# Two graph layers on one core: four walk blocks instead of three, first-walk rows on GpSimd's queue, the last row pair by halves, and layer-1 pools split by place

## The chip, the cores and the metric

The kernel runs on one core of one Trainium2 chip. Its time is the device time of one execution in microseconds (us). The engines are named as in the profile: PE is TensorE's matmul side and PEld its weight loads, DVE is VectorE, ACT is ScalarE, POOL is GpSimd, and SP is SyncE, which only issues DMAs. ACT and POOL can issue DMAs too, from queues of their own.

## The reference, cut to what matters

The input is `x` (2708 rows of 256) and a sparse 2708 x 2708 matrix `adj`. Two layers follow each other.

```python
# layer 0, two steps n = 0, 1
R = adj + eye(N);  R = R / R.sum(-1)                  # a row-stochastic walk matrix
A  = top_p_attention(Xa, W1, W2, W3)                  # softmax of q k^T, cut to the 0.9 nucleus, renormalised
Xf = R @ Xf                                           # the walk
Xa = A @ Xa                                           # the attention
Z += Xf @ U1[n].T + Xa @ U2[n].T
x  = layernorm(x + layernorm(X + Z) * g + b)
# layer 1: graph attention, 4 heads of 64
e  = leaky_relu(s_i[:, None] + s_j[None, :])          # masked where adj (with its diagonal) is 0
x  = layernorm(x + softmax(e) @ Wh)
```

Each walk is a dense product of the 2708 x 2708 matrix with 256 columns, each attention step makes the scores, searches the cut of the nucleus in every row, transposes the probabilities and multiplies them with 256 columns, and layer 1 is a masked product of the same size for four heads.

## The kernel before, in words

The 2708 rows are 22 row tiles: 16 of 128 rows and 6 of 110. Two neighbouring tiles make a pair, so there are 11 pairs (`PAIRS`).

**The walk** (`walks`, from line 1021) does the product of one pair of row tiles with all columns in seven phases, a Strassen scheme of 2 x 2 blocks (Winograd's form). Each phase multiplies one block matrix of 11 tiles (`D11`, `S2`, `A12`, `S3`, `S1`, `D22`, `S4`; `A12` comes from `adj`, the others were mixed during the first attention step and lie in DRAM) with one half of the columns (`B11`, `T2`, `B21`, `T3`, `T1`, `T4`, `B22`). A phase is 11 products, which the trace shows as 22 matmul instructions. A phase's block is 704 KB. The buffers of the blocks come from the pool `adjp`, which has three; the block of phase `at + 2` is requested when phase `at` begins (line 1067), into the buffer of phase `at - 1`. SP issues these transfers (line 681, `get`; line 669 for `A12`, `fetch`). There are 77 phases in the first walk and 77 in the second.

The operands `B..` and `T1` lie in `xe`, the terms `T2`, `T3` and `T4` in `xm`, which held the layer's input until the first attention step was done with it. A column of ones in `xe` and one in `t2` give the row sums: in the first walk the phases 0 to 2 are 129 columns wide, and lines 1090 and 1094 take the reciprocals. Lines 1086 to 1102 take each phase's sum out of PSUM, some on ACT, most on DVE. Two PSUM banks (`walk0`, `walk1`) change turns, so phase 4 of a pair can begin when ACT has copied phase 2's result (line 1092), phase 5 when DVE has added phase 3's (line 1096), and the next pair's phase 0 when DVE has added phase 5's (line 1100).

When a row tile of the first walk is done, `after_walk0` (line 1143) scales it and adds a term on POOL (lines 1146, 1148), and SP stores it to DRAM (line 1149, `xmd`). The term (`ca`) is fetched by SP (line 1046, in `beside`), asked for in phase 3. The last pair is not stored: POOL writes it straight into `xe` (line 1151), both halves of the columns of both tiles, after the pair's phase 6. `return_rows` (line 1114) brings the other rows from `xmd` into `xe` in three parts, as the operands come free. `reblend` (line 1130) then makes `T3`, `T2` (DVE, lines 998 and 1000), `T1` and `T4` (POOL, lines 1002 and 1004) for the second walk. The second walk's phase 0 waits in the program's order for both tiles of the last pair to be written, and its later phases for the blends.

**The attention** (`step`, line 1252) goes row tile by row tile. Each has six groups of up to four 128-column parts: a transpose on PE (line 258), a copy on ACT (line 263, `eT`), a product (line 276, `att`). After each group `slot` (line 1237) advances the other work by one step: the search for the cut of later rows (lines 787 to 960: exponentials and counts on ACT, a short chain of one-column operations on POOL from line 794 to 840, the sorting on DVE), what follows finished rows, and then up to 12 products of the walk. Between the two attention steps there is a stretch in which slots run one after another with 14 products each (line 1367 and 1372): there the walk runs without attention beside it.

The program writes out the order of PE, ACT, DVE and POOL by hand (`manual_schedule` with those four engines), so each of these engines does its instructions in the order of the program text. SP is not among them: a planner orders its DMAs by when it reckons that they can start, and SP then works through that list one by one. An SP transfer whose wait isn't over holds everything behind it.

`finish` (line 1206) ends a row tile of the second walk: it stores the row (line 1222, `xd`) and then runs `sources` (line 158), which makes layer 1's values and stores them (line 183, `v`). For the last three tiles it puts their first term into `x_late` (line 1049), behind a small POOL memset (line 1042).

**Layer 1** (`layer1`, line 1446) takes the same buffers over: its pools open when layer 0's pools close. In each of three spans (1024, 1024 and 660 columns) it goes over the 22 tiles `j`: the mask block of `j` comes by SP (line 238, `neighbours`, into `adjp`), ACT makes it 0 or 1 (lines 239 and 240, Sign and Square), DVE makes the weights `pt` for four heads (line 1540, four instructions), and PE multiplies (line 1552 values, line 1562 denominators). The pool `pj` holds the weights of three `j`, `ps_v` the six PSUM banks of the sums, `keep1` the 22 value tiles. The first two masks are asked for in the last attention tile, after its group 4 (line 1278, `early`). Layer 1's stretched-out rows of the span (`e<-shared`, `r<-shared`) come by lines 216 and 224. At `(g, i) == (0, 12)` SP brings the rows stored in `xd` back into `xe` (line 1615, 2 MB and 330 KB), for the residual sum that begins in the second span.

Of the kernel before, what the change touches and what calls it, by code (L numbers as in the profile page):

```python
# [45 lines left out]
def kernel(  # L46
# [57 lines left out]
    nc.gpsimd.memset(xe[:, :, HALF : HALF + 1], 1.0)  # L104
# [439 lines left out]
    def fast_layer0(ep, adjp):  # L544
# [89 lines left out]
        p1, y1, y2 = (spare_u[:, k * (HALF + 1) : (k + 1) * (HALF + 1)] for k in range(3))  # L634
        u_rows = u_sb[:, 1].rearrange("p c s d -> p (c s) d")
        lines = [u_rows[:, k, :] for k in range(4)]
        lines += [spare_u[:, c : c + D] for c in (3 * HALF + 3, 3 * HALF + 3 + D)]
# [338 lines left out]
        def halves_of(t, m):  # L976
# [5 lines left out]
        t2 = flat[:, PAIRS * HALF : PAIRS * (D + 1)].rearrange("p (j c) -> p j c", c=HALF + 1)  # L982
        t4 = flat[:, PAIRS * (D + 1) : PAIRS * (D + 1 + HALF)].rearrange(
            "p (j c) -> p j c", c=HALF
        )

# [5 lines left out]
        def blend(name, j0, j1, k):  # L992
# [3 lines left out]
            u3, u2, u4 = t3[:k, j0:j1], t2[:k, j0:j1, 0:HALF], t4[:k, j0:j1]  # L996
# [13 lines left out]
            "T1": lambda j, k, w: xe[:k, 2 * j, second],  # L1010
            "T2": lambda j, k, w: t2[:k, j, 0:w],
# [9 lines left out]
        def walks():  # L1021
# [6 lines left out]
            def load(s, i, n):  # L1028
                blk = new_block(rows[2 * i])
                key = PHASES[n][0]  # L1030
                if key == "A12":
                    fetch(blk, 2 * i, 1)
                else:
                    get(key, i, blk)
                return blk

            def beside(s, t):
# [7 lines left out]
                if not s:  # L1045
                    nc.sync.dma_start(ca[:m], c1[t][:m])
                    return ca, None
# [9 lines left out]
            blocks = [load(*queue[0]), load(*queue[1])]  # L1057
            walking.append(True)
            yield
            for at, (s, i, n) in enumerate(queue):  # L1060
# [3 lines left out]
                while s and (unfinished or (n and blending)):  # L1064
                    yield True
                blk = blocks.pop(0)
                if at + 2 < len(queue):
                    blocks.append(load(*queue[at + 2]))
# [5 lines left out]
                if n == 3:  # L1074
                    aside = {t: beside(s, t) for t in (a, b)}
                w = HALF + 1 if s == 0 and n < 3 else HALF
                ac = use[bank][:m, :w]
                for j in range(PAIRS):
# [5 lines left out]
                    if j == PAIRS - 1:  # L1084
                        if n == 0:
                            nc.scalar.copy(p1[:m, :w], ac)
                        elif n == 1:
                            nc.vector.tensor_add(y1[:m, :w], ac, p1[:m, :w])
                            if s == 0:
                                nc.vector.reciprocal(rinv[:m, b : b + 1], y1[:m, HALF : HALF + 1])  # L1090
                        elif n == 2:
                            nc.scalar.copy(xa[:m, :HALF], ac[:, :HALF])
                            if s == 0:
                                nc.vector.reciprocal(rinv[:m, a : a + 1], ac[:, HALF : HALF + 1])
                        elif n == 3:
                            nc.vector.tensor_add(y2[:m, :HALF], ac, p1[:m, :HALF])
                        elif n == 4:
                            nc.vector.tensor_add(xb[:m, HALF:], ac, y2[:m, :HALF])
                        elif n == 5:
                            nc.vector.tensor_add(xb[:m, :HALF], ac, y2[:m, :HALF])  # L1100
                        else:
                            nc.vector.tensor_add(xa[:m, HALF:], ac, y1[:m, :HALF])
                        for t, xw, last in ((b, xb, 5), (a, xa, 6)):
                            if n == (6 if (s, i) == (0, PAIRS - 1) else last):
                                if s == 0:
                                    unfinished.add(t)
                                doing.append((after_walk0, finish)[s](t, xw[:m], *aside[t]))
                                next(doing[-1])
                        if (s, i) == (0, PAIRS - 1) and n in (2, 4, 6):
                            return_rows(n)  # L1110
# [3 lines left out]
        def return_rows(n):  # L1114

            odd, cols = {2: (None, slice(0, HALF)), 4: (0, second), 6: (1, second)}[n]
# [9 lines left out]
            if n == 6:  # L1126
                blending.append(True)
                doing.append(reblend())

        def reblend():  # L1130
# [3 lines left out]
            while unfinished:  # L1134
# [8 lines left out]
        def after_walk0(t, xw, ca, _):  # L1143
# [3 lines left out]
            if t < NT - 2:  # L1147
                nc.gpsimd.tensor_add(xw, xw, ca[:m])
                nc.sync.dma_start(xmd[:m, t], xw)
            else:  # L1150
                nc.gpsimd.tensor_add(
                    halves_of(t, m), xw.rearrange("p (h c) -> p h c", h=2),
                    ca[:m].rearrange("p (h c) -> p h c", h=2),
                )
            unfinished.remove(t)
# [50 lines left out]
        def finish(t, xw, ca, cb):  # L1206
# [12 lines left out]
            if not late:  # L1219
                yield  # L1220
                yield from norms(t, xt, ca)
                nc.sync.dma_start(xd[:m, t], xt)
                yield from sources(t, rowp, free_bank, src=xt)


        going, doing, unfinished, stored = [], [], set(), set()
        early, walked, blending, begun = [], [], [], []
# [24 lines left out]
        def step(s, cur, spend):  # L1252
            turned_first = None
            for t in range(NT):
# [11 lines left out]
                def between(n):  # L1266
# [11 lines left out]
                    if s and (t, n) == (NT - 1, len(groups) - 2):  # L1278

                        early.extend(neighbours(0, j, adjp) for j in first[:2])  # L1280
                    if (s, t) == (0, NT - 1):
# [4 lines left out]
                        if n == 2:  # L1286
                            nc.gpsimd.memset(t2[:, :, HALF : HALF + 1], 1.0)
# [158 lines left out]
    def layer1(ep, adjp, r=None, verdict=None, early=()):  # L1446
        l1 = ExitStack()

        pp, rp, pj, keep = (
            l1.enter_context(tc.tile_pool(name=name, bufs=bufs))  # L1450
            for name, bufs in (("pp", 2), ("rp", 1), ("pj", 1), ("keep1", 1))
        )
        DEEP = 3
# [284 lines left out]
```

## Time and profile before

| | |
|---|---|
| median of 3 runs | 1554.12 us (1552.58 to 1556.42) |
| profiled execution, its own time | 1554.5 us |
| its span | 1552.5 us |
| PE busy | 1496.7 us (96%) |
| DVE busy | 1297.9 us (84%) |
| ACT busy | 800.4 us (52%) |
| POOL busy | 611.0 us (39%) |
| mean granted TensorE clock | 0.987 |

The span lies 2 us below the time of the same execution, so a difference of spans can be read as a difference of times. PE is busy nearly all the time, which makes its few idle stretches the thing to look at, together with the stretches in which its clock was granted at half. The stages, by the times at which their lines run: the first attention step with the mixing of the blocks up to 440 us, the walk alone to 521 us, the second attention step with the rest of the first walk up to 790 us and with the second walk from there to 1197 us, the last attention groups to 1205 us, and layer 1 to the end.

Columns of the profile's lines: a wait is "who waited, for whom: us in total, times, longest". A timeline line is "start, duration, engine, line, operation, out<-in, shape, count, [idle time before it, and what ended it]". A line that counts several instructions starts with the first and ends with the last.

### The profile page before, as it was taken

The numbers are of one execution on the slowest core, as the hardware profiler recorded it, in microseconds if no ns is written. First come the engines' busy times: TensorE is split into PE (matmuls) and PEld (weight loads), VectorE is DVE, ScalarE is ACT, GpSimd is POOL, SyncE is SP. The second block draws the span as 40 slices with busy tenths as digits, with TensorE's granted clock in tenths as the row PEclk, the third lists the DMA queues.
The fourth block names the chain that finished last, engine by engine and source line by source line (L and its number), as shares of the span: only waits on it lengthen the run. The fifth ranks groups of instructions, "written<-read, shape, count | busy, mean of one in ns | idle before, by whom it ended". The sixth has DMA issues, their size and how long they took to land.

```text
span 1552.5 us, 29929 instructions
## 1 busy us (share of the span) xinstructions
PE 1496.7 (96%) x10537; PEld 1068.9 (69%) x10537; DVE 1297.9 (84%) x3763; ACT 800.4 (52%) x1472; POOL 611.0 (39%) x1016
## 2 busy tenths in 40 slices
PE   8999999999998999999989999999998999999995
PEld 4477777777787889988878888888887323333342
DVE  4599999999525878888889998999893998999995
ACT  3444444444335456656645666666641444456474
POOL 2267777865023223222343454545432220035133
PEclk9999999999998999999999999999999999999998
DMA  6198988894037655544555555555556445334331
GB/s 171 57 273 260 287 272 260 263 260 154 12 117 221 182 163 160 172 154 143 168 157 167 173 175 172 183 164 157 146 169 198 123 118 169 96 106 132 86 108 46
DMA packets 208010, 255.97 MB, mean 165 GB/s; under 512 B 42151, under 2 KB 171949, under 8 KB 207851
## 3 DMA queue, kind: packets, MB, share of 16 engines
q1 hardware_dynamic: 198042, 239.68, 51.4%
q0 software_dynamic: 3648, 9.26, 1.9%
q10 hardware_dynamic: 6161, 5.03, 1.1%
q8 instruction: 85, 1.39, 0.4%
q14 instruction: 74, 0.61, 0.1%
HBM read 190.10 MB, written 62.44 MB: 163 GB/s over the span
## 4 chain that ended last, share of the span: by engine, by line
PE 83%; DVE 8%; POOL 3%; ACT 2%; DMA 2%; issue 2%; ACTq 0%; DVEq 0%; SPq 0%; POOLq 0%
PE att L276 24%; PE walk L1080 20%; PE acc L1552 11%; PE lg L783 7%; PE tr L258 6%; PE acc L1562 6%; DVE pt L1540 3%; PE walk L1181 2%; PE walk L1197 2%; DMA blk<-S 1%; PE walk L753 1%; PE lg L170 1%; DVE top L906 1%; DVE work L908 1%; ACT junk L808 1%
## 5 line engine op out<-in xcount | busy, mean ns | idle before, releaser
L808 ACT ACTIVATE junk<-e,minus,rth 128x2708 bf16<-128x2708 f32 (+1 forms) x88 | 232.9, 2647 | 49.7 <-POOL rth L840 48.9
L1080 PE MATMUL walk<-xe,blk 128*128 128x128 f32 (+7 forms) x1936 | 242.4, 277 | 12.5 <-DMA blk<-S 4.6
L263 ACT COPY eT<-tr 128x512 f32<-128x512 f32 (+5 forms) x264 | 141.4, 536 | 218.4 <-PE tr L258 215.8
L1080 PEld LDWEIGHTS walk<-xe,blk 128*128 128x128 f32 (+3 forms) x1936 | 230.7, 188 | 28.6 <-issue 16.8
L276 PE MATMUL att<-ba,eT 128*128 128x256 f32 (+3 forms) x968 | 231.3, 380 | 0.0
L276 PE MATMUL att<-xm,eT 128*128 128x256 f32 (+3 forms) x968 | 230.8, 379 | 0.3 <-ACT xa L1270 0.3
L1552 PE MATMUL acc<-pt,v 128*32 128x512 f32 (+3 forms) x2112 | 218.3, 547 | 3.7 <-ACT xa L1270 3.1
L1080 PE MATMUL walk<-xm,blk 128*128 128x128 f32 (+6 forms) x1452 | 188.0, 280 | 7.8 <-DMA blk<-S 6.3
L1540 DVE SCALAR_TENSOR_TENSOR pt<-e,tj,blk 128x1024 f32<-128x1024 f32 (+3 forms) x176 | 184.4, 1113 | 10.6 <-PE att L276 7.8
L1080 PEld LDWEIGHTS walk<-xm,blk 128*128 128x128 f32 (+3 forms) x1452 | 178.0, 191 | 20.9 <-issue 12.5
L276 PEld LDWEIGHTS att<-ba,eT 128*128 128x128 f32 (+3 forms) x968 | 170.2, 187 | 21.5
L276 PEld LDWEIGHTS att<-xm,eT 128*128 128x128 f32 (+3 forms) x968 | 169.6, 186 | 22.0 <-ACT xa L1270 0.7
L787 ACT ACTIVATE e<-lg 128x1024 f32<-128x1024 f32 (+1 forms) x132 | 121.0, 921 | 112.9 <-PE lg L783 107.0
L1552 PEld LDWEIGHTS acc<-pt,v 128*32 128x32 f32 (+1 forms) x2112 | 70.6, 110 | 136.0 <-issue 111.3
L258 PE MATMUL tr<-ident,e 128*128 128x128 f32 (+3 forms) x968 | 148.3, 272 | 4.0 <-ACT eT L263 4.0
L258 PEld LDWEIGHTS tr<-ident,e 128*128 128x128 f32 (+3 forms) x968 | 112.0, 139 | 46.2 <-issue 26.7
L1562 PE MATMUL acc<-pt,sb 128*32 128x512 f32 (+3 forms) x1056 | 112.8, 542 | 0.0
L1540 DVE SCALAR_TENSOR_TENSOR pt<-r,tj,blk 128x1024 f32<-128x1024 f32 (+1 forms) x88 | 109.9, 1313 | 1.2 <-issue 0.6
L888 DVE MAX8 cand<-scr 128x8 f32<-128x97 f32 (+1 forms) x616 | 102.9, 247 | 0.0
L888 DVE MAX8 cand<-e 128x8 f32<-128x170 f32 (+1 forms) x352 | 85.8, 323 | 20.4 <-ACT e L787 20.3
L239 ACT ACTIVATE blk<-blk 128x1024 f32<-128x1024 f32 (+3 forms) x66 | 63.2, 959 | 75.5 <-DMA blk<-in_adjT_dram 65.9
L906 DVE MAX8 top<-work 128x8 f32<-128x128 f32 (+3 forms) x242 | 82.4, 340 | 8.3
(265 smaller groups left out, 2206.4 us busy)
## 6 DMA issues: line engine op xcount, KB each, us to landing
blk<-in_adjT_dram SPq DMA_DIRECT2D x72, 512.0 KB
blk<-S SPq DMA_DIRECT2D x64, 512.0 KB
blk<-D SPq DMA_DIRECT2D x32, 512.0 KB
blk<-in_adjT_dram SPq DMA_DIRECT2D x27, 440.0 KB
blk<-S SPq DMA_DIRECT2D x64, 165.0 KB
blk<-S SPq DMA_DIRECT2D x24, 440.0 KB
D<-blk SPq DMA_DIRECT2D x16, 512.0 KB
S<-scr SPq DMA_DIRECT2D x16, 512.0 KB
```

Source lines behind the costliest of these rows:

```text
L258: nc.tensor.transpose(tr[: rows[t], q, :m], e[:m, off[t] : off[t + 1]], ident[:m, :m])
L263: copy(eT[:k, : len(grp), :m], tr[:k, : len(grp), :m])
L276: nc.tensor.matmul(acc, eT[: rows[t], q, :m], value(t), start=(t == 0), stop=(t == NT - 1),)
L783: nc.tensor.matmul(lg[:m, h, :w], qT[part, cols], kT[s][part, c0 : c0 + w], start=True, stop=True,)
L787: nc.scalar.activation(halves[:m, :, c0 : c0 + w], lg[:m, :, :w], AF.Exp, accum_out=zp[:m, n : n + 1],)
L808: nc.scalar.activation(junk[:m], e[:m], func, scale=rth, bias=minus1[:m], accum_out=acc)
L888: nc.vector.max(cand[:, n, :], src[:m, n * size : min(N, (n + 1) * size)])
L906: nc.vector.max(top[:, k : k + 8], work if k else flat)
L1080: nc.tensor.matmul(ac, blk[:k, j, :], MOVING[name](j, k, w), start=start and j == 0, stop=j == PAIRS - 1, skip_group_check=True,)
L1540: nc.vector.scalar_tensor_tensor(pt[:k, :gw], targets[g][h // 2][:k, h % 2, :gw], tj[:k, j, h : h + 1], bar, op0=ALU.max, op1=ALU.mult,)
L1552: nc.tensor.matmul(acc[h // 2][c][to : to + SIDE, :w], v[j][:k, h, o : o + SIDE], probs[n][h][:k, c0 : c0 + w], **at,)
L1562: nc.tensor.matmul(acc[2][c][h * SIDE : (h + 1) * SIDE, :w], sb[:k, j, h : h + 1].to_broadcast([k, SIDE]), probs[n][h][:k, c0 : c0 + w], **at,
```

## The change

- **Four walk blocks, three ahead.** `t2` loses its column of ones, so `t3`, `t2` and `t4` fill three quarters of `xm`, and the last quarter is a fourth block buffer (`fourth`), taken by every fourth phase. The block of phase `at + 3` is requested when phase `at` begins.
- **Row sums.** `xe` gets a second column of ones behind its second half. The row sum of the odd tile comes with phase 4 (`S1`, `T1`) instead of phase 1, so the phases 0, 2 and 4 are 129 wide, and that tile's reciprocal is taken after phase 4. `p1`, `y1`, `y2` lose their extra column.
- **First-walk rows by GpSimd's queue.** The term's load (now in phase 0 of the pair) and the store to `xmd` are issued by POOL, 22 and 20 DMAs.
- **The last pair by halves.** `last_rows` scales and adds each half of each of the last two tiles as it is done (after phases 2 and 5, and both second halves after phase 6). The second walk's phase 0 waits only for the first halves; later phases still wait for the blends.
- **`finish`** stores `xd` after `sources` instead of before it.
- **Layer 1.** `pj` becomes three pools of one, `ps_v` six pools of one bank, and the first four value tiles get a pool of their own (`keep2`), so each waits for what lay in its own place. The two early masks are asked for after group 3 instead of group 4. A small POOL memset on `xe` is put ahead of the transfers of line 1615.

```diff
     xe = const.tile([P, NT, D + 2], F32, name="xe")
-    nc.gpsimd.memset(xe[:, :, HALF : HALF + 1], 1.0)
+    for one in (HALF, D + 1):
+        nc.gpsimd.memset(xe[:, :, one : one + 1], 1.0)
...
         t3 = flat[:, : PAIRS * HALF].rearrange("p (j c) -> p j c", c=HALF)
-        t2 = flat[:, PAIRS * HALF : PAIRS * (D + 1)].rearrange("p (j c) -> p j c", c=HALF + 1)
...
+        t2, t4 = (
+            flat[:, k * PAIRS * HALF : (k + 1) * PAIRS * HALF].rearrange("p (j c) -> p j c", c=HALF)
+            for k in (1, 2)
         )
+        fourth = flat[:, 3 * PAIRS * HALF :]
...
             def load(s, i, n):
-                blk = new_block(rows[2 * i])
+                if (s * PAIRS * 7 + i * 7 + n) % 4 == 3:
+                    blk = compact(fourth, rows[2 * i])
+                else:
+                    blk = new_block(rows[2 * i])
...
                 if not s:
-                    nc.sync.dma_start(ca[:m], c1[t][:m])
+                    nc.gpsimd.dma_start(ca[:m], c1[t][:m])
                     return ca, None
...
-            blocks = [load(*queue[0]), load(*queue[1])]
+            AHEAD = 3
+            blocks = [load(*queue[at]) for at in range(AHEAD)]
...
-                while s and (unfinished or (n and blending)):
+                while s and (owing & {(t, 0) for t in (NT - 2, NT - 1)} or (n and blending)):
                     yield True
                 blk = blocks.pop(0)
-                if at + 2 < len(queue):
-                    blocks.append(load(*queue[at + 2]))
+                if at + AHEAD < len(queue):
+                    blocks.append(load(*queue[at + AHEAD]))
...
-                if n == 3:
+                if n == (3 if s else 0):
                     aside = {t: beside(s, t) for t in (a, b)}
-                w = HALF + 1 if s == 0 and n < 3 else HALF
+                w = HALF + 1 if s == 0 and n in (0, 2, 4) else HALF
...
+                        if (s, i) == (0, PAIRS - 1):
+                            if n in (2, 4, 6):
+                                return_rows(n)
+                            for t, xw, h in {
+                                2: ((a, xa, 0),), 5: ((b, xb, 0),), 6: ((b, xb, 1), (a, xa, 1))
+                            }.get(n, ()):
+                                owing.add((t, h))
+                                doing.append(last_rows(t, xw[:m], aside[t][0], h))
                                 next(doing[-1])
...
             nc.gpsimd.tensor_scalar(xw, xw, rinv[:m, t : t + 1], None, op0=ALU.mult)
...
+            nc.gpsimd.tensor_add(xw, xw, ca[:m])
+            nc.gpsimd.dma_start(xmd[:m, t], xw)
+            rows_kept.append(t)
+
+        def last_rows(t, xw, ca, h):
+            m, cols = rows[t], slice(h * HALF, (h + 1) * HALF)
+            yield
+            nc.gpsimd.tensor_scalar(
+                xw[:, cols], xw[:, cols], rinv[:m, t : t + 1], None, op0=ALU.mult
+            )
+            nc.gpsimd.tensor_add(halves_of(t, m)[:, h, :], xw[:, cols], ca[:m, cols])
+            owing.remove((t, h))
...
                 yield from norms(t, xt, ca)
+                yield from sources(t, rowp, free_bank, src=xt)
                 nc.sync.dma_start(xd[:m, t], xt)
-                yield from sources(t, rowp, free_bank, src=xt)
...
-                    if s and (t, n) == (NT - 1, len(groups) - 2):
+                    if s and (t, n) == (NT - 1, len(groups) - 3):
 
                         early.extend(neighbours(0, j, adjp) for j in first[:2])
...
-        pp, rp, pj, keep = (
+        DEEP = 3
+        pp, rp, *pj, keep, keep_first = (
             l1.enter_context(tc.tile_pool(name=name, bufs=bufs))
-            for name, bufs in (("pp", 2), ("rp", 1), ("pj", 1), ("keep1", 1))
+            for name, bufs in (
+                ("pp", 2), ("rp", 1), *((f"pj{k}", 1) for k in range(DEEP)),
+                ("keep1", 1), ("keep2", 1),
+            )
         )
...
-        ps_v = l1.enter_context(tc.tile_pool(name="ps_v", bufs=1, space=PSUM))
+        ps_v = [
+            [
+                l1.enter_context(tc.tile_pool(name=f"ps_v{k}{c}", bufs=1, space=PSUM))
+                for c in range(2)
+            ]
+            for k in range(3)
+        ]
...
-            v[t] = keep.tile([P, H, FO], F32, name=f"v{t}")
+            v[t] = (keep_first if t in first[:4] else keep).tile([P, H, FO], F32, name=f"v{t}")
...
             if fast and (g, i) == (0, 12):
+                nc.gpsimd.memset(xe[:, 0 : NT - LATE, 0:1], 0.0)
                 for t0, t1 in ((0, 16), (16, NT - LATE)):
                     nc.sync.dma_start(
                         xe[: rows[t0], t0:t1, 0:D], xd[: rows[t0], t0:t1, :]
```

## The prediction

> **What bounds the kernel now.** I read the page first. PE is busy for 96% of the span, no other engine for more than 84%, and the chain that ended last runs 83% over PE. So only PE's idle time, and time at a lower clock, can be won, as long as no other engine is close behind. Next I read PE's waits, and the timeline of PE around each long one.
>
> ```profile
> PE walk L1080 <- DMA blk<-S: 10.9, 3, 4.6
> PE walk L1080 <- POOL xe L1151: 4.6, 1, 4.6
> PE acc L1552 <- ACT xa L1270: 3.1, 1, 3.1
> ```
>
> The three transfers of a block `S` ended PE's waits at 471.56, 495.82 and 1185.32 us; the other two waits lie at 793.00 and 1205.14. Each has a second price. In a table of stretches (length, then busy time of PE, PEld, DVE, ACT and POOL, PE clock, DMA share, GB/s) the clock behind each is half:
>
> ```profile
> 474.40:477.70 3.30, 3.30 (x17) 3.30 (x17) 0.00 (x0) 2.35 (x2) 0.00 (x0) 0.50 0.89 284
> 498.30:505.00 6.70, 5.04 (x23) 5.07 (x24) 5.45 (x22) 4.55 (x5) 0.00 (x0) 0.50 0.92 301
> 795.30:802.00 6.70, 4.40 (x18) 4.25 (x19) 5.03 (x11) 0.79 (x3) 6.13 (x5) 0.50 0.45 141
> 1187.80:1194.50 6.70, 4.58 (x21) 4.59 (x22) 0.00 (x0) 0.03 (x1) 0.00 (x0) 0.50 0.48 175
> 1208.30:1211.60 3.30, 3.30 (x16) 0.71 (x20) 3.30 (x3) 0.81 (x1) 2.79 (x2) 0.50 0.14 31
> ```
>
> Then I asked why the block was late at 495.82. The timelines of SP, PE and ACT around it:
>
> ```profile
> 493.35 2.04 SPq L1149 DMA_DIRECT2D xmd<-xw  x2
> 495.50 1.67 SPq L681 DMA_DIRECT2D blk<-S  x4
> ...
> 493.20 2.62 PE L1080 MATMUL walk<-xe,blk 128*128 128x129 f32 x22
> 499.96 5.04 PE L1080 MATMUL walk<-xm,blk 128*128 128x128 f32 x22 [4.14 <-DMA blk<-S]
> ...
> 497.32 2.64 ACT L808 ACTIVATE junk<-e,minus,rth 128x2708 bf16<-128x2708 f32 x1 [3.48 <-POOL rth L840]
> 499.97 0.24 ACT L1092 COPY xw<-walk 128x128 f32<-128x128 f32 x1
> ```
>
> SP sits in the store of a finished row until POOL has made it (495.04) and only then issues the block. A phase of 22 products takes 2.62 us, and 5.04 at half clock. The ACT lines matter below. At the end of the walk SP shows the same, behind `x_late` and the spread of layer 1's rows, and then DVE:
>
> ```profile
> 1176.29 0.30 SPq L1049 DMA_DIRECT2D x_late<-in_x_dram  x1
> 1176.68 0.76 SPq L681 DMA_DIRECT2D blk<-D  x2
> 1177.53 0.31 SPq L1049 DMA_DIRECT2D x_late<-in_x_dram  x1
> 1177.96 1.01 SPq L224 DMA_DIRECT2D e<-shared  x2
> 1179.38 3.13 SPq L681 DMA_DIRECT2D blk<-S  x2
> ...
> 1205.23 10.54 DVE L1540 SCALAR_TENSOR_TENSOR pt<-e,tj,blk 128x1024 f32<-128x1024 f32 x8 [7.79 <-PE att L276]
> ```
>
> From 1205.23 to 1287 DVE has no gap (80.28 of 81 us busy), and PE's pairs of `j` begin 12.0 to 12.9 us apart in places against 10.3 later: this stretch is DVE's, and ends earlier by as much as `pt` starts earlier.
>
> **The change, place by place**
>
> *First walk, 460 to 516 us.* Leaving the SP queue, the 20 stores release 38.2 us of SP's waits for POOL (line 1149), and a block asked for three phases ahead has 7.9 us instead of 5.2 (phases of 2.62). I take both block waits as gone. If nothing else were late, that is 2.14 + 4.14 of idle and half of the half-clock work (3.30 and 5.04), 4.2: 10.5 us, with the 0.83 wait at 515.53 11.3. But phase 4 needs ACT's copy of line 1092, which stands behind the count of line 808, which waits for POOL's `rth`. POOL's chain to `rth` stands behind two finished rows (491.57 to 495.04), and now also behind their two stores, 0.57 us each on POOL by line 1204 (0.55 to 0.65 for the same size in the trace). In the first pair `rth` comes 1.1 to 1.4 later, so phase 4 starts at about 475.6 instead of 477.85: 2.2 won. In the next pair the whole chain starts 2.2 earlier and pays 1.1: ACT's copy at 499.2, phase 4 at 499.4 instead of 504.79. DVE then becomes the pacemaker: its reciprocal at line 1094 comes after that copy (it waited for ACT all 8 times listed, 17.1 us), and behind it lie 3.8 (line 954), 0.3, 0.3, 3.03 (957), 1.8 and 3.06 us (873) before line 1100 frees the bank for the next pair: 512.4 instead of 516.1. **I take 3.7 us.** From 516 to 790 PE is busy for 272.23 of 274 us, so it is carried on. Bounds: 11.3, if the chain gives way, and 1.6, if all four DMAs of a pair stand ahead of the chain at the trace's longest, 0.80 us (line 759): 3.2 instead of 1.1. A loss is rival 3. The 22 loads of the term cost POOL as much, but fall into its idle time at a pair's start (461.2 to 464.4), and are needed seven phases later.
>
> A rule speaks against this part. The Trainium skill ("DMA: Bandwidth & Descriptors", section "Issuing engines are not separate DMA queues") says that issuing from several engines saves only the sequencer's issue time. By that the stores would be worth 0.33 us of SP each and nothing to PE, and the sum would be 10.6 instead of 14.3. The rows above show another thing that is saved, the wait for data at the head of a queue, so I go by the rows.
>
> *The row sums* change which phases are 129 wide, not how many; one reciprocal (0.16 us of DVE) moves by three phases. A memset of 0.12 us goes. Nothing, under PE's 2.62 us phases.
>
> *Between the walks, 790 us.* PE did 20 of phase 0's 22 products and waited 4.60 us for the last pair; phase 1 began at 798.19. With the halves phase 0 runs through, ending at 793.1. Phase 1 needs `T2`, whose first part DVE ended at 795.95: it waited for the returned rows at 793.05 (line 998, 1.23 us) and took 1.63 more (line 1000). That part is not changed, so a wait of 2.9 us takes the place of 4.6. Phase 1 starts 2.2 earlier. Of half clock PE paid 4.40 us, that is 2.2; after 2.9 idle I expect a stretch of 3.4 us and pay 1.3, as after 2.14 and 3.08 us of idle above. The four half-size operations end on POOL by about 795, in time. **3.1 us**; bounds 0 (both parts late) and 6.8 (no wait, no half clock).
>
> The Trainium skill ("TensorE: Matmul & The Clock Gate", section "What's actually happening") lets the clock fall after an idle window of about 3.4 us. This trace drops it after waits of 2.14 and 3.08 us. By the page the 1.3 would not be paid and the sum would be 15.6; I go by the trace.
>
> *End of the walk and start of layer 1, 1176 to 1287 us.* The last two blocks are asked for one phase (some 4.6 us) earlier, ahead of `x_late` and the spread, so 0.82 + 4.61 idle and half of 4.58 go: 7.7 us. The first `pt` could start at 1197.5 by that. It starts when the first mask is ready. With the masks one group earlier ACT does Sign and Square right after the copy at 1201.55 (less 7.7, 1193.8 plus 0.54): ready after 2 x 1.06 at 1196.5. The place allows it, if pools are laid out in the order in which they open: layer 1 has some 42 KB a partition ahead of the first `pj` (16 KB), layer 0 some 40 ahead of `xm` (22 KB), so the first `pj` lies over `xm`, the second over the rest of it and `qT`, which are done by then, and only the third over `ba`, which the last attention product reads. So `pt` starts at 1196.5, 8.7 us earlier. The price: the last group's `eT` copy now stands behind four mask operations (4.3 us) and PE's last four products come some 2.5 late, which costs nothing, because DVE sets the pace from there. Bounds: 1.0, if the block stays late and only the mask's move counts (1205.23 less 7.7, against 1196.5), and 8.7, since the mask sets the start. PE's wait of 3.08 and its half clock lie under it too. What is behind those masks on ACT is that copy and PE; what is behind SP's mask transfers is the third mask.
>
> *The reload of `xe`.* Line 1615 held SP from 1186 to 1193.68. It now waits for a POOL memset that comes with the last of POOL's line 1585, about 1268, next to the spread of the second span's rows (1281 to 1286, 2 MB). In that spread a mask took 7.4 us (1286.45 to 1293.85 on ACT) instead of 3.5 (1210.58 to 1214.10), and DVE waited 2.62 us. Another 2.3 MB at the 280 GB/s of the page's busiest slices is 8.4 us. A mask has about 4 us to spare (two `j` of 4.9, less 3.5 and 2.1). **I take 1.5 us lost**, between 0 and 8.
>
> `finish` storing `xd` later unblocks SP (18.8 us of waits at line 1222), where PE waited for no block: nothing. If a row's `xd` is later, it is needed 70 us on.
>
> Sum: 3.7 + 3.1 + 8.7 - 1.5 = **14.0 us**. The profiled execution took 1554.5, 0.4 above the median; from the median it is **1540 us**.
>
> **Rivals**
>
> 1. *All stalls go and nothing takes their place*: 11.3 + 6.8 + 8.7, no loss at the reload: 1527. For it: the waits are single events. Against it: ACT's 3.48 us behind POOL. 13%.
> 2. *The order of SP's list keeps the last block behind the spread, or the reload collides*: the end brings 1.0 instead of 8.7, or the reload costs 8: 1548 or 1547, and 1554 with both. For it: `blk<-D` stood behind `x_late` although its buffer was long free. 20%.
> 3. *POOL becomes the walk's pacemaker, and the kernel slower.* Two stores and two loads per pair, 2.3 us of POOL, lie ahead of `rth`, and ACT's `eT` copies stand behind the count that waits for `rth`. If a copy comes later than the 1.89 us that the group's product lasts, PE stalls in each of 9 pairs; at 2.3 us and a half-clock loss of 1.7 each it costs 36, and the time is 1554 + 36 - 14 = 1576. It decides from 1.6 us a pair. Against it: in the attention ACT waited for `rth` with 0.27 us (528.82) and PE had no gap in 274 us. 7%.
> 4. *No change*: DVE, 91% busy from 940 to 1160 us (200.22 of 220), turns what PE wins into waits for rows of the search. 5%.
>
> **How the numbers follow.** My forecast, 1534 to 1546, gets 55%. The range leaves out the lower end of rival 1, and 3 and 4: 1530 to 1551. 0.3% of this time (4.7 us) is about what a measurement of it can tell: faster 0.86 (forecast, rival 1, most of rival 2), the same 0.07, slower 0.07.
>
> **What would show it.** Right: no wait of line 1080 for `blk<-S`; lines 1149 and 1046 gone from SP's waits; one wait near 790 below 3.5 us, for DVE's line 1000; `pt` starting before the last attention product has ended; three half-clock stretches fewer. Wrong: waits of PE for ACT's `eT` between 516 and 790, or gaps of DVE and ACT for masks after the reload.

## The result

The changed kernel took 1558.62 us (median of 10 runs), the kernel before 1555.42 (10 runs beside them): 1.0026 times the time before, 95% interval 1.0016 to 1.0036. It is slower by some 3 us, where 1540 had been forecast. The profiled execution took 1558.56 us with a span of 1556.7 (1552.5 before).

Both traces hold the same number of matmul instructions (10537), so the place of the k-th one in the two traces shows where time was won and lost. The table cuts the span where PE did the same work in both; times on the left are those of before, the other numbers microseconds gained (−) or lost (+) within the stretch. The last column is the first experiment below, with the first walk's rows issued by SP again.

| stretch (us of before) | predicted | after | after, rows on SP |
|---|---|---|---|
| start, to 81 | 0 | +0.95 | +1.82 |
| 81 to 466, first attention | 0 | 0.0 | 0.0 |
| 466 to 542, first walk | −3.7 | **+2.83** | **−6.43** |
| 542 to 753 | 0 | +0.40 | −0.08 |
| 753 to 868, between the walks | −3.1 | −0.86 | −0.82 |
| 868 to 1157 | 0 | +0.68 | +0.72 |
| 1157 to 1199, end of the walk, start of layer 1 | −8.7 | −8.17 | −8.16 |
| 1199 to 1349, reload of `xe` | +1.5 | +2.36 | +1.16 |
| 1349 to the last product | 0 | 0.0 | 0.0 |
| behind the last product | 0 | **+6.03** | +0.34 |
| span | −14.0 | +4.2 | −11.5 |

The first row varied from +0.4 to +2.4 over the traces of kernels that are the same there, so a single trace tells about 1 us. The row between the walks varied from −0.9 to +0.9 where the kernels are the same there, with the places of the half-clock stretches. The table names the two places that spoil the sum: the first walk and the time behind the last product.

PE's waits of the kernel after (us in total, times, longest):

```profile
PE walk L1086 <- DVE rinv L1108: 5.5, 2, 3.8
...
PE walk L1086 <- DVE xm L1002: 2.8, 1, 2.8
PE walk L1086 <- DVE xw L1105: 2.4, 1, 2.4
PE acc L1578 <- DVE pt L1566: 2.3, 1, 2.3
```

No wait for a block is left, and none for POOL's last rows. In their place stand waits for DVE: in the first walk for a reciprocal (`rinv`), between the walks for line 1105 and for `T2`. The reciprocal is the end of a chain that begins on POOL. POOL and then ACT in the first of the two long waits (start, duration, operation, idle time before it and its releaser):

```profile
466.39 0.94 POOL L1159 TENSOR_SCALAR xw<-xw,rinv 128x256 f32<-128x256 f32 x1
467.42 0.72 POOL L1160 TENSOR_TENSOR xw<-xw,ca 128x256 f32<-128x256 f32 x1
468.44 0.70 POOL L1161 DMA_DIRECT2D xmd<-xw  x1 [0.30 <-POOL xw L1160]
469.14 1.09 POOL L1051 DMA_DIRECT2D ca<-c  x2
470.26 0.94 POOL L1159 TENSOR_SCALAR xw<-xw,rinv 128x256 f32<-128x256 f32 x1
471.28 0.72 POOL L1160 TENSOR_TENSOR xw<-xw,ca 128x256 f32<-128x256 f32 x1
472.30 0.61 POOL L1161 DMA_DIRECT2D xmd<-xw  x1 [0.30 <-POOL xw L1160]
472.94 0.20 POOL L835 TENSOR_TENSOR kept<-kept,over 128x1 f32<-128x1 f32 x1
...
475.08 0.19 POOL L841 TENSOR_TENSOR rth<-rth,g 128x1 f32<-128x1 f32 x1
```

```profile
475.30 2.64 ACT L809 ACTIVATE junk<-e,minus,rth 128x2708 bf16<-128x2708 f32 x1 [7.08 <-POOL rth L841]
477.85 0.19 ACT L809 ACTIVATION_READ_ACCUMULATOR junk<-e,minus,rth 128x1 f32 x1
477.94 0.24 ACT L1097 COPY xw<-walk 128x128 f32<-128x128 f32 x1
```

`rth` is the value of the search that ACT's next count takes in. Two stores, each with a wait of 0.30 us for the row just made, and both loads of the next pair's `ca` stand between the rows and the chain to `rth`. ACT waits for `rth` 7.08 us (3.96 before), its copy comes at 477.94, then DVE's reciprocal, and PE has idled 3.81 us. The stretches of that place (length, busy time of PE, PEld, DVE, ACT, POOL, PE clock, DMA share, GB/s) show what follows the idle time:

```profile
474.60:478.05 3.45, 0.03 (x1) 0.00 (x0) 0.00 (x0) 2.75 (x3) 0.59 (x2) 1.00 0.98 309
478.05:484.90 6.85, 6.46 (x19) 3.70 (x20) 4.13 (x13) 4.07 (x6) 0.00 (x0) 0.50 0.18 59
```

Behind the last product, ACT had made the last output row at 1543.08 us, 1.8 earlier than before (1544.89). The program's end did not follow, because of a closing instruction of POOL's queue. The instructions of the kernel's last line, first of before, then of after (count, then shortest, median and longest in ns):

```profile
L1734 POOLq DRAIN  x3: 40/107/6685, 1544.9 to 1552.2; - x3
```

```profile
L1761 POOLq DRAIN  x3: 40/106/10115, 1545.7 to 1556.4; - x3
```

The long DRAIN grew from 6.69 to 10.12 us. Before the change POOL issued 81 DMAs, after it 123: 82.5 and 82.2 ns for each. POOL also came to it later: between its branch on the last flag and the next instruction lay 0.4 us before the change (1544.44 to 1544.87) and 3.0 after it (1542.63 to 1545.65). 3.4 and 2.6 are the 6.0 us of the table.

### The profile page after: what moved, and what is told of

The parts are those of the page before. It is cut to its first block, busy times and chain, and to the rows that moved or that the text cites. A ratio compares the mean times of both kernels' runs of the same rounds, so it can differ in the third digit from the quotient of the medians.

```text
span 1556.7 us, 29932 instructions
## 1 busy us (share of the span) xinstructions
PE 1496.2 (96%) x10537; PEld 1068.6 (69%) x10537; DVE 1295.4 (83%) x3763; ACT 801.1 (51%) x1472; POOL 642.4 (41%) x1063
## 5 line engine op out<-in xcount | busy, mean ns | idle before, releaser
L1086 PE MATMUL walk<-xe,blk 128*128 128x128 f32 (+6 forms) x1452 | 180.8, 275 | 7.0 <-DVE xw L1105 2.4
L1086 PEld LDWEIGHTS walk<-xe,blk 128*128 128x128 f32 (+3 forms) x1452 | 172.0, 187 | 17.2 <-issue 7.2
L1086 PE MATMUL walk<-xm,blk 128*128 128x128 f32 (+3 forms) x1100 | 140.9, 278 | 4.5 <-DVE xm L1002 2.8
L1086 PEld LDWEIGHTS walk<-xm,blk 128*128 128x128 f32 (+3 forms) x1100 | 133.0, 189 | 14.4 <-issue 7.8
```

The source lines that it names most:

```text
L1086: nc.tensor.matmul(ac, blk[:k, j, :], MOVING[name](j, k, w), start=start and j == 0, stop=j == PAIRS - 1, skip_group_check=True,)
```

## The experiments

All medians are set against the kernel before, run beside them (1555.0 to 1555.8 us). "Rows on SP" is the first kernel below. The lines of the next three are against the kernel after, or against the kernel just before them where that is said; from "POOL's order or its DMA path?" on, each kernel is an edit of rows on SP.

**Only the queue undone.** My theory Q was that POOL's queue costs both losses; the rival R was that the tail comes from layer 1's pools or the place of the code.

```
-                    nc.gpsimd.dma_start(ca[:m], c1[t][:m])
+                    nc.sync.dma_start(ca[:m], c1[t][:m])
...
-            nc.gpsimd.dma_start(xmd[:m, t], xw)
+            nc.sync.dma_start(xmd[:m, t], xw)
```

> The kernel after, with the 22 loads and 20 stores of the first walk's rows issued by SP again, as before the change. Theory Q (the queue): POOL's DMAs cost twice. POOL's closing DRAIN took 6.68 us with 81 DMAs issued by POOL and 10.12 us with 123, 0.082 us for each, so it is 6.7 again with 81; and without two loads and two stores ahead of rth, ACT's copy for phase 4 of the first pairs is no longer 3 us late. SP waits for finished rows again, but its blocks are fetched three phases ahead (7.9 us against waits of up to 3.8), so at most one short wait of PE for a block returns. 1558.6 - 3.4 - (0 to 4) = 1551 to 1555. Rival R (the tail is longer for another reason: the six accumulator pools of layer 1, or the place of POOL's code): the DRAIN stays near 10.1 and the time at 1558.6, or above it if PE waits for blocks as before.

Measured: 1542.89 us, ratio 0.9926 (0.9913 to 0.9940). The DRAIN is 6.69 us again. POOL and ACT in the same place (this trace starts 0.87 us later than that of after):

```profile
467.27 0.94 POOL L1159 TENSOR_SCALAR xw<-xw,rinv 128x256 f32<-128x256 f32 x1
468.30 0.73 POOL L1160 TENSOR_TENSOR xw<-xw,ca 128x256 f32<-128x256 f32 x1
469.01 0.93 POOL L1159 TENSOR_SCALAR xw<-xw,rinv 128x256 f32<-128x256 f32 x1
470.03 0.73 POOL L1160 TENSOR_TENSOR xw<-xw,ca 128x256 f32<-128x256 f32 x1
470.71 0.19 POOL L835 TENSOR_TENSOR kept<-kept,over 128x1 f32<-128x1 f32 x1
...
472.85 0.19 POOL L841 TENSOR_TENSOR rth<-rth,g 128x1 f32<-128x1 f32 x1
```

`rth` comes 3.1 us earlier (475.08 less 472.85, and the 0.87), and PE's wait there is 0.71 us instead of 3.81. Q stands. R falls for the DRAIN; for the 2.6 us by which POOL came to it late, the place of its code stays possible. And I had put the gain far too low (1551 to 1555): the two spans differ by 15.7 us, 9.3 in the first walk, 5.7 behind the last product and 1.2 at the reload, less 0.5 elsewhere. Of the 9.3, 5.9 is idle time of PE (9.75 us in that stretch against 3.80) and 3.4 is half of the longer half-clock time (10.24 us against 3.41). And no wait of PE for a block came back, although SP again stood before its stores until POOL had made the rows (SP's waits, us in total, times, longest):

```profile
SPq L1161 <- POOL xw L1160: 39.6, 17, 4.0
```

**The loads alone back on SP.**

```
-                    nc.gpsimd.dma_start(ca[:m], c1[t][:m])
+                    nc.sync.dma_start(ca[:m], c1[t][:m])
```

> The kernel after, with only the 22 loads of ca back on SP; the 20 stores stay with POOL. Theory Q: 101 DMAs by POOL, so a closing DRAIN of 8.3 us (1.8 less than 10.12); rth comes 1.1 us earlier in each pair than in the kernel after, of which PE keeps 1 to 3 us with the half clock. 1558.6 - 1.8 - 1 to 3 = 1554 to 1556. Rival R: DRAIN 10.1, 1558.6.

Measured: 1553.37 us, ratio 0.9989 (0.9980 to 0.9998), a little under the range. The first walk stands at −0.63 (after +2.83, rows on SP −6.43): of the 9.3 us the loads cost 3.5, somewhat more than the 1 to 3 expected, and the stores 5.8. With 101 DMAs the DRAIN takes what Q said:

```profile
L1761 POOLq DRAIN  x3: 40/107/8318, 1543.9 to 1552.8; - x3
```

**The stores by SP, one slot later**, so that SP finds the row ready.

```
             nc.gpsimd.tensor_add(xw, xw, ca[:m])
-            nc.gpsimd.dma_start(xmd[:m, t], xw)
+            yield
+            nc.sync.dma_start(xmd[:m, t], xw)
```

> The kernel after, with the loads on SP, and the stores on SP too, but written one slot later than the POOL operations that make the row, so that SP should find it ready. Theory Q: DRAIN 6.7, no POOL DMA ahead of rth and no wait of SP for the row, so the first walk has neither loss: 1558.6 - 3.4 - 4 to 7 = 1548 to 1551. If SP's waits for rows never reached PE with three blocks ahead, it equals the run with the rows on SP and no delay. Rival R: 1558.6, DRAIN 10.1.

Measured: 1544.14 us, ratio 0.9931 (0.9918 to 0.9945), not better than rows on SP; the first walk gives −6.5 in both. SP's waits for rows do not reach PE.

**No DMA by POOL at all.** As the kernel just before, and the other 81 DMAs by ACT (two of the four places shown).

```
-                nc.gpsimd.dma_start(qT[here, lo:hi], qT[there, lo:hi])
+                nc.scalar.dma_start(qT[here, lo:hi], qT[there, lo:hi])
...
-            nc.gpsimd.dma_start(c2[t][:m], cs[:m])
+            nc.scalar.dma_start(c2[t][:m], cs[:m])
```

> As the run before it (rows on SP, stores one slot later), and the other 81 DMAs of POOL (q turned across halves, the three terms' stores) are issued by ACT, which makes their data. Theory Q: nothing to settle for POOL at the end, so its DRAIN falls to under 1 us and SP's own closing (5.1 us behind the last store in the trace before) sets the end: 5 to 6.6 us less tail than the kernel after. ACT issues a DMA in 0.33 us, 27 us in all, with 48% of its time idle: between nothing and 4 us of it reach PE. 1545 to 1551. Rival R: the DRAIN stays, and ACT's issues only add: 1558 to 1562.

Measured: 1555.12 us, ratio 1.0001 (0.9992 to 1.0010), above the 1545 to 1551 expected. The end gains more than expected (8.0 us on the kernel after, where 5 to 6.6 had been said), and the long DRAIN is gone:

```profile
L1762 POOLq DRAIN  x3: 34/50/82, 1549.6 to 1552.3; - x3
```

But PE was 13.3 us later by 282 us than in the kernel just before, 2.0 of it in the first 81 us. In the first attention it waits for ACT's copies (7.2 us in three waits, the longest 3.9), and two of the waits have 3.4 us of half clock behind them. Ahead of 120 us ACT idled 6.3 us, with its DMA of `qT` at 119.69 and the copy PE needs behind that. I had priced an issue at 0.33 us (measured 0.29 to 0.84 over the 81) and left out what stands behind it.

**POOL's order or its DMA path?** One plain POOL operation per row in place of the store.

```
             nc.gpsimd.tensor_add(xw, xw, ca[:m])
+            nc.gpsimd.tensor_scalar(xw, xw, 1.0, None, op0=ALU.mult)
             nc.sync.dma_start(xmd[:m, t], xw)
```

> The run with the rows on SP (1542.89 us), and one more POOL operation per finished row, xw times 1.0 (0.94 us as line 1159, in place of the 0.61 to 0.70 us of a store and its 0.30 wait); no DMA on POOL's queue is added. Theory O (POOL's order): a store costs the walk because rth stands behind it, whatever it is. Then this kernel loses in the first walk what the run with the loads alone on SP lost there, 5.8 us between 466 and 542 us, with a wait of PE of 2 to 3 us near 477 and one more half-clock stretch, and the closing DRAIN is 6.7: 1548 to 1550. Rival P (the path): the loss is in how POOL's queue carries the bytes (late landing, descriptors); then a plain operation costs at most the 1 us of PE's existing slack: 1543 to 1544.

Measured: 1551.01 us, ratio 0.9972 (0.9962 to 0.9981). Two operations of 0.86 us put `rth` 1.8 us later (the stores alone put it 2.1 later), and the first walk gives −1.14 instead of −6.43: 5.3 us lost, near the 5.8 of the stores, with no DMA added. So for the stores it is POOL's order, not the path of the bytes; for the loads, which stand in the same list, that is concluded from the stores. (The trace is of an execution of 1553.88 us. It also gives 3.2 us more at the reload, 1.4 between the walks and 2.2 behind the last product, where the DRAIN starts 2.5 late.)

**How many blocks ahead.**

```
-            AHEAD = 3
+            AHEAD = 2
```

> The run with the rows on SP, its blocks fetched two phases ahead instead of three (four buffers stay). Theory B: the third block ahead is what takes SP's waits for rows off PE. Then PE waits for blocks again near 472 and 494 us (2.1 and 4.1 before the change) and at the end of the walk near 1176 (4.6), with half clock behind them: 6.5 us in the first walk and 5 to 8 at its end, 1549 to 1557. Rival: the loads of ca, moved to the start of a pair, and the halves did it, and the third block nothing: 1542 to 1544.

Measured: 1543.78 us, ratio 0.9928 (0.9916 to 0.9940); first walk −6.5, no wait for a block. My theory B fell: with four buffers, the third fetch ahead does nothing by itself.

**Three buffers.** Fetched two ahead, and no block in `xm`.

```
-                if (s * PAIRS * 7 + i * 7 + n) % 4 == 3:
-                    blk = compact(fourth, rows[2 * i])
-                else:
-                    blk = new_block(rows[2 * i])
+                blk = new_block(rows[2 * i])
```

> The run with the rows on SP, two blocks fetched ahead and no fourth block in xm, so three buffers as before the change. The run with two ahead and four buffers lost nothing, so by theory F the fourth buffer is what takes SP's waits off PE: SP no longer has to wait for PE to leave a block before it fetches the next, whatever the place in its list. Then PE's waits for blocks return near 472, 494 and 1176 us: 6.5 us in the first walk and 5 to 8 at its end, 1553 to 1557. Rival M: the moved loads of ca and the later store of xd freed SP's list, and the buffer did nothing: 1542 to 1545.

Measured: 1558.37 us, ratio 1.0023 (1.0013 to 1.0033). All the waits for blocks are back, and the end of the walk gains nothing (+0.2 from 1157 to 1199, against −8.2):

```profile
PE walk L1083 <- DMA blk<-S: 10.3, 3, 4.1
```

(PE's waits.) Theory F stands: against the run with two ahead the buffer is worth 14.6 us. How it does it shows in SP's list near the second long wait. SP with four buffers and two ahead, and in the second fence with three:

```profile
486.64 0.76 SPq L682 DMA_DIRECT2D blk<-S  x2
491.51 2.04 SPq L1161 DMA_DIRECT2D xmd<-xw  x2
```

```profile
493.76 2.05 SPq L1158 DMA_DIRECT2D xmd<-xw  x2
495.91 1.67 SPq L682 DMA_DIRECT2D blk<-S  x4
```

With four buffers SP issues the block of `S3` ahead of the pair's two stores. With three it comes behind them, and PE waits 3.95 us for it. The planner's list is not the same in the two kernels, so the buffer and the order that it allows were not told apart.

**Layer 1's pools in one piece each** (`pj` and `keep1` shown, `ps_v` likewise).

```
-                ("pp", 2), ("rp", 1), *((f"pj{k}", 1) for k in range(DEEP)),
-                ("keep1", 1), ("keep2", 1),
+                ("pp", 2), ("rp", 1), ("pj", 1), ("keep1", 1),
```

> The run with the rows on SP, with layer 1's probabilities, values and accumulators in one pool each, as before the change; the masks stay one group earlier. Theory L: the separate pools let pt start while the last attention product still reads the rows under them. With one pool pt starts behind that product, 1 to 6 us later than at 1192.0, and PE waits 2 to 4 us with half clock behind it: 1544 to 1549. Rival: the masks one group earlier and the early blocks did it, and the pools nothing: 1542 to 1544.

Measured: 1548.67 us, ratio 0.9962 (0.9949 to 0.9974). DVE's first `pt` waits for the last attention product, as theory L said. Groups of DVE around the start of layer 1 (busy time and mean ns, then idle time before and its releaser), with one pool and, in the second fence, with the pools apart:

```profile
L1559 DVE SCALAR_TENSOR_TENSOR pt<-e,tj,blk 128x1024 f32<-128x1024 f32 x16 | 20.2, 1329 | 11.9 <-PE att L277 11.9
```

```profile
L1566 DVE SCALAR_TENSOR_TENSOR pt<-e,tj,blk 128x1024 f32<-128x1024 f32 x18 | 22.9, 1340 | 7.5 <-ACT blk L241 7.5
```

That start costs PE 4.1 us (1157 to 1234), the reload another 2.6 here. All three kinds of pool were undone together; the line shows it for `pt`, and which of them counts was not tried.

**The masks one group later.**

```
-                    if s and (t, n) == (NT - 1, len(groups) - 3):
+                    if s and (t, n) == (NT - 1, len(groups) - 2):
```

> The run with the rows on SP, with the first two masks of layer 1 written one group later in the last attention row, as before the change; the pools stay apart. Prediction's step: the first mask sets the start of pt. Then pt starts 2 to 4 us later than at 1192.0 and the time is 1544 to 1547. Rival: by then pools and blocks decide, and pt waits for nothing else: 1542 to 1543.5.

Measured: 1543.89 us, ratio 0.9932 (0.9919 to 0.9945): `pt` starts 1.2 us later, where 2 to 4 had been expected, and PE is 0.9 later at 1234 us. The median lies between the two ranges that I gave, and 1.0 us is about what two medians can tell apart. The trace names a transfer of `v`, not the mask, as what `pt` waited for.

**T4 ahead of T1.** Between the walks PE waited 2.76 us for the second part of `T2`, which DVE makes from `T3`. DVE and POOL in the kernel after:

```profile
802.02 2.70 DVE L1000 TENSOR_TENSOR xm<-xe 110x384 f32<-110x384 f32 x1 [3.75 <-POOL xe L1170]
804.76 0.56 DVE L1002 TENSOR_TENSOR xm<-xm,xe 110x384 f32<-110x384 f32 x1
```

```profile
801.94 2.37 POOL L1004 TENSOR_TENSOR xe<-xe 128x1024 f32<-128x1024 f32 x1
```

The same size takes 0.56 us on the second line and 2.70 on the first, which ends 0.4 after POOL's operation. The edit to `reblend`:

```
-            for name in ("T1", "T4"):
+            for name in ("T4", "T1"):
```

> The run with the rows on SP, with POOL's T4 written ahead of its T1 between the walks. DVE's second part of T3 took 2.70 us beside POOL's T1 of 2.37 (before the change the first part, more than twice as large, took 1.23 alone). Theory S: the two engines hold each other up on SBUF; T4 needs T2, so POOL waits, T3 takes 0.6, and PE's wait of 2.77 us for T2 falls to 0.7 or less, with the half clock behind it (1.7): 1539 to 1541. Rival: T3's length is its own, or T1 and T4 are then late for phases 4 and 5: 1543 or above.

Measured: 1542.20 us, ratio 0.9922 (0.9909 to 0.9934). PE's wait was 2.35: POOL's first operation was now T4's large part, which needs nothing of the second part either, and T3 took 2.33 beside it. The edit had missed its aim, so it was made again:

```
-            for name in ("T1", "T4"):
-                for part in J_PARTS:
+            for name in ("T4", "T1"):
+                for part in J_PARTS[::-1]:
```

> The run with the rows on SP, with POOL's T4 ahead of T1 and of each the second, small part first, which needs T2's second part. In the run with T4 first POOL still began with a part that needs nothing (793.17 to 795.17) and DVE's small part of T3 again ended 0.42 behind it, after 2.34 us. Theory S (an operation of DVE on two tensors does not run beside POOL's): now POOL has to wait for DVE, T3's part takes 0.56, and PE's wait falls from 2.35 to 2.8 to at most 0.7: 1539.5 to 1541.5. Rival: the part is long for itself, behind POOL's row: its 2.3 to 2.7 us stay, and the wait grows: 1543 to 1545.

Measured: **1539.80 us, ratio 0.9900 (0.9885 to 0.9915)**, the fastest kernel of the study, and faster than both. POOL now waits for DVE, and DVE's part takes what its size asks for:

```profile
795.09 0.56 DVE L1000 TENSOR_TENSOR xm<-xe 110x384 f32<-110x384 f32 x1 [5.09 <-POOL xe L1170]
795.68 0.56 DVE L1002 TENSOR_TENSOR xm<-xm,xe 110x384 f32<-110x384 f32 x1
```

```profile
796.32 2.83 POOL L1006 TENSOR_TENSOR xm<-xe,xm 110x384 f32<-110x384 f32 x2 [1.26 <-DVE xm L1002]
```

PE's wait is 0.62, and 753 to 868 gives −3.3 instead of −0.82; none of the kernels with the old order was better than −0.9 there. The Trainium skill ("SBUF — State Buffer", section "Terms") says that VectorE and GpSimd share a pair of ports that one holds for a whole instruction while the other is blocked; these rows agree (0.56 alone, 2.70 beside 2.37).

**All at once.** The last edit, the third term's 18 stores by ACT, and the reload of `xe` six products earlier.

```
-                            nc.gpsimd.dma_start(c3[t][:m], xa[:m])
+                            nc.scalar.dma_start(c3[t][:m], xa[:m])
...
-            if fast and (g, i) == (0, 12):
+            if fast and (g, i) == (0, 6):
```

> The run with the rows on SP, and three edits together: T4 ahead of T1 with its small part first, as in the run on that; the 18 stores of the third term by ACT, which makes them, so 63 DMAs by POOL and a closing DRAIN of 5.2 us instead of 6.7; and the reload of xe six products earlier, at about 1225 us, away from the spread of the second span's rows. If each brings what its rows say (2.1, 1.5, and 1 to 2 of the 1.2 to 4.3 us that PE loses near 1285 to 1300): 1537.5 to 1539. If ACT's issues or the earlier reload reach the masks: 1540 to 1545.

Measured: 1544.07 us, ratio 0.9930 (0.9917 to 0.9943), 4.3 us behind the kernel without the last two edits. The DRAIN is 5.22 us with 63 DMAs, as expected, but POOL came to it 2.5 us late (3.0 us behind its branch). The early reload met something else: PE lost 4.1 us between 1264 and 1294 us of before, with a new wait and 3.4 us of half clock behind it, against 1.5 at the old place. The stores by ACT cost PE nothing (0.6 from 868 to 1157, 0.7 without). PE's wait:

```profile
PE aux L165 <- ACT xe L1618: 1.8, 1, 1.8
```

## Why the prediction was wrong

**The step that failed: "In the first pair `rth` comes 1.1 to 1.4 later ... I take 3.7 us", and the loads that "fall into its idle time at a pair's start".** The chain was named rightly, down to the copy on ACT and DVE's reciprocal, and sized wrongly. A store cost POOL 0.61 to 0.70 us and a wait of 0.30 for its own row, not 0.57; and the loads, written at the next pair's first phase, stood in POOL's list ahead of the chain and added 1.09. `rth` came 3.1 us later. The walk paid about three times the delay: with 0, 1.8, 2.1 and 3.1 us of it the first walk gave −6.4, −1.1, −0.6 and +2.8, because the delay comes in two pairs and half clock follows the waits. I had taken 1.6 us won as the bound for four DMAs ahead of the chain; it was a loss of 2.8. Rival 3 named POOL as the pacemaker, but expected it to cost in the attention's groups, where PE lost 0.4 us (542 to 753); it cost in the two pairs where nothing but the walk was left for PE.

**A term that was missing: POOL's closing DRAIN**, 82 ns for each DMA that POOL has issued (0, 63, 81, 101 and 123 DMAs: 0.08, 5.22, 6.69, 8.32 and 10.12 us). The trace of before had the 6.69 us behind the last output row, and I had not read past the last computing instruction. The 42 DMAs moved cost 3.4 us, and POOL's late start on the DRAIN 2.6, whose cause stays open.

**"Leaving the SP queue, the 20 stores release 38.2 us of SP's waits" and "a block asked for three phases ahead has 7.9 us".** The outcome was right, the reason wrong. With the stores on SP, and with two fetched ahead, PE waits for no block; with three buffers it does. The fourth buffer did it, and with it in place moving the stores brought PE nothing; whether the move would have helped with three buffers was not tried. There the Trainium skill's rule that I set aside ("DMA: Bandwidth & Descriptors", "Issuing engines are not separate DMA queues") gave the better answer for PE, though SP's waits for rows are real (39.6 us).

**Between the walks** 3.1 was forecast and 0.9 came. "Phase 0 runs through" failed: without the gate it stands 2.2 us earlier in PE's list, behind no attention group, and its bank is the one that the last phase used; it waits 2.36 us for line 1105, which DVE does behind 3.04 us of line 874. The wait for `T2` was there as forecast (2.76 for 2.9), but for its second part, which POOL held up. The new wait, 2.36 for the 0.29 that stood there before, is most of the 2.2 that are missing.

**End of the walk and start of layer 1** was right: −8.2 for −8.7, with `pt` at 1200.80 and the trace 4.0 late, so at 1196.8 where 1196.5 was said. What it needed most were the blocks (8.3 lost without the buffer) and the pools apart (4.1); the masks' place, which I had made the setter of the start, weighs 0.9. **The reload** was within its bounds: 2.4 lost (1.5 said), and 1.1 to 4.3 in the other kernels with the reload at this place.

Without the queue edit the sum of the terms up to the last product holds: 13.6 won behind the first 81 us, 14.0 said. That is luck: the first walk's −6.4 (−3.7 said) makes up for the −0.8 between the walks (−3.1 said). The halves of the last pair, the moved row sums and the later store of `xd` were not undone one by one.

Three slips of the working changed nothing. By the terms of its own sum, "10.6 instead of 14.3" should read 10.3 instead of 14.0, and 15.6 should read 15.3. And 471.56, 495.82 and 1185.32 us, like 793.00 and 1205.14, are the times at which PE's waits began; they ended 2.1 to 4.6 us later.

## What to carry to other kernels

Before a DMA moves to an engine that also computes, read what stands behind it in that engine's list and who ends up waiting: here 2 to 3 us per pair on an engine busy 39% of the time cost PE about three times as much in one walk. Read the profile past the last computing instruction too, since what an edit leaves to be settled there is paid in full. When a change gives a stream of transfers more buffers, an earlier request and a new queue, test them apart: the buffer was worth 15 us, the earlier request nothing, and the new queue cost 16 (1558.62 less 1542.89).

## What was not expected of the hardware

- POOL's last DRAIN takes 82 ns for each DMA that POOL issued, in a straight line from 0 to 123 DMAs.
- Behind the branch on the last flag POOL went on after 0.4 us in the kernels with 1016 or 1021 POOL operations (DMAs counted in) and after 2.9 to 3.1 in those with 940, 1003, 1041 and 1063. That it depends on where POOL's code lies is a guess; no run changed that alone.
- A DVE operation on two tensors of 110x384 took 0.56 us alone and 2.3 to 2.7 beside a POOL operation on two tensors, ending 0.4 behind it.
- A wait of PE of 1.75 to 1.78 us for the same product (line 1095's result) was followed by 3.4 us of half clock in the kernel after, with the rows or the loads on SP and with the later masks, and by none in the others whose wait was as long (late stores, no DMA by POOL, two ahead, one pool, T4 first in both forms, all at once). What decides it was not tried.
